# Four chained vision layers on one core: softmax sums partly by accumulating transfers, and inverse roots taken on compact tiles by way of memory

## The chip, the cores and the metric

The kernel runs on one core of one Trainium2 chip. The metric is the device time of one execution in microseconds. The core has a matrix engine (PE, with its weight loads shown apart as PEld), a vector engine (DVE), an activation engine (ACT), a general engine (POOL), and a sync engine (SP) that here does nothing but issue transfers. Each engine runs its own instructions strictly in the order in which the program lists them; they meet through semaphores. SBUF is the working memory, PSUM the eight banks into which PE writes, and DRAM the memory outside the core.

## What is computed

The input is 16 frames of 384 channels by 16 by 16 pixels, as two batches of eight frames. Four layers follow each other. All is in float32.

```python
# layer 0: attention of 12 heads of 32 channels over N = 2048 tokens of a batch
attn = softmax(einsum('bhnd,bhmd->bhnm', q * scale, k), axis=-1)
attn = alpha * eye + beta * attn - gamma * Cm        # Cm = 1/N everywhere
out = einsum('bhnm,bhmd->bhnd', attn, v)             # v is the input itself
# layer 1: 7x7 depthwise convolution, LayerNorm over channels, 384->1536, gelu,
y = (y - mu) * rsqrt(var + 1e-6) * ln_g + ln_b
y = gelu(y @ w1 + b1, approximate=False)
gx = sqrt(sum(y * y, axis=(1, 2)))                   # of each channel and frame
nx = gx / (mean(gx, axis=-1) + 1e-6)
y = (grn_g * (y * nx) + grn_b + y) @ w2 + b2         # 1536->384, and + residual
# layer 2: two Sobel filters, 768->384, LayerNorm, gelu, + residual
# layer 3: 1x1, 3x3 depthwise, 1x1, linear attention with phi(t) = exp((2t - t*t)/2),
#          projection, then LayerNorm, 384->1536, gelu, 1536->384, + residuals
```

## The kernel before

**Tiling.** A batch's 2048 tokens are four blocks of 512 (`BLK`). An activation is a tile of 128 partitions by 3 by 512. An attention *unit* is a batch and a group of four heads, so there are six units, each with four blocks of queries: 24 *blocks*. A block has 16 *steps* (`NQC`), one for every 128 keys.

**A step** (`unit`, lines 456 to 559). `scores` (463) makes four matmuls `st`, one per head, that run in four row groups of PE at the same time, and ACT takes their exponential into `e`. PSUM holds three double banks for this (`pst`, 412), so one ACT instruction covers two heads (1024 columns) and there are two of them in a step. `weighted` (481) is run one step later: four matmuls `av` multiply `e` by the values into one bank; DVE adds `e` to a running sum `s` (two `tensor_tensor` of 1024 columns). The sum over the 128 partitions is a matmul with ones, `dn`. How many steps DVE adds up before a `dn` is given for each block by `ADDS` (55): 16 means that DVE adds the whole block and PE makes one `dn`; 4 means four groups in a block, and all groups but the last are spread over later steps in four parts of 128 columns. `e` has 8 buffers of two heads and `s` has 4.

**The end of a block.** ACT copies `av` to `va`, and `xg` from the input. `finish` (536) reads `dn` with ACT into `r`; `due` then holds, for steps 2 to 5 of the next block, four reciprocals of 128 columns on DVE, at 6 and 7 the scaling and the store into the layer's output `l`, at 8 a check of the inverses on ACT. In step 5 (`SLOT`) of a block, `project` (569) makes two of the projections `p` that give queries and keys: six matmuls each, then an ACT copy.

**What fills the gaps.** `fill` (1481) is called after every step. It puts work of layer 1 among the attention's instructions: the convolution (49 DVE instructions per chunk, tile `y`) and the first parts of two layer 1 blocks ("leads"). `pace` (194) is a table by which it reckons what PE and DVE have in a step.

**The tail.** After attention, a planner (`Plan.all`, 180) puts all remaining work in one static order: it knows for every operation an engine, a length, what it comes after, and buffers; `RANK` (46) orders the tasks and `SLACK` (52) lets a better rank start later. `TURNS` (36) says which blocks use which pair of MLP weights one after the other; at every turn new weights (three tiles `wa`, three `wb`, 768 KB each) are loaded by SP.

**Normalizations.** `scaled` (916) makes the channel sum of squares by a matmul `sv` with ones, so that all 128 partitions hold the same row of 512 numbers; ACT takes the square root of 128x512, DVE the reciprocal of 128x512 in place, and DVE multiplies. It is called 24 times: by `layer1` (1012), `layer2` (1141) and `layer3c` (1421) for each of eight blocks. `layer1` also takes the root of `gx` (128x24) on ACT. ACT keeps one set of function tables at a time; roots, gelu and exp are in different sets here, and a load of tables stands between them.

Of the kernel before, what the change touches and what calls it, by code (L numbers as in the profile page):

```python
# [13 lines left out]
PSUM = bass.MemoryType.PSUM  # L14

# [16 lines left out]
SLOT = 5  # L32
# [4 lines left out]
    (0, ((0, 0), (0, 1), (0, 2), (0, 3),)),  # L37
    (1, ((0, 0), (0, 1),)),
    (0, ((1, 0), (1, 2),)),
    (1, ((0, 2),)),  # L40
    (0, ((1, 1), (1, 3),)),
    (1, ((1, 0), (0, 3), (1, 2), (1, 1), (1, 3),)),
# [4 lines left out]
    "mid": ((36.6, 22.0, 24.3, 85.6), (18.6, 42.9, 96.6, 26.9)),  # L47
    "l1": ((50.1, 89.5, 75.2, 4.0), (51.1, 16.8, 81.7, 28.5)),
    "l3c": ((45.7, 99.2, 100.9, 121.0), (-20.9, -6.3, 70.9, 62.0)),
    "conv": 109.4,  # L50
}
SLACK = 0.196
JUNK = 2

ADDS = (16, 8, 16, 16, 4, 4, 4, 2, 2, 8, 16, 16, 4, 16, 2, 4, 16, 8, 4, 4, 4, 4, 4, 4)
# [61 lines left out]
class Plan:  # L117
# [24 lines left out]
    def run(self, op):  # L142
        at = self.start(op)
        assert at is not None
        for tag, n in op.takes:
            del self.room[tag][:n]
        if op.engine == "PE" and at - self.free_at["PE"] > 2:
            at += 1.5
        if op.engine:
            self.free_at[op.engine] = at + op.length  # L150
        op.ready = at + op.length + op.lag
        for tag, n in op.gives:
            self.room[tag] = sorted(self.room[tag] + [op.ready] * n)
        if op.makes:
            self.made[op.makes] = op
        self.table = op.table or self.table
# [37 lines left out]
def pace(t):  # L194
# [3 lines left out]
    adds = ADDS[n]  # L198
    pe, dve = 2.066, 2.275 if t and i % adds else 0.0
    at = i - adds - 1  # L200
    parts = sum(j * adds // 4 == at % adds for j in range(4)) if at >= 0 else 0
    if parts:
        pe += 0.22 * parts
    elif i == 1 and n > 0:
        pe += 0.87
    else:
        pe += 0.09
    if n > 0:
        dve += {2: 0.88, 3: 0.88, 4: 0.88, 5: 0.88, 6: 0.6, 7: 0.66}.get(i, 0.0)
# [188 lines left out]
def attention(tc, X, xt, L0, block, small, col, cols, ones, load_qk, banks, fill, bound):  # L398
# [6 lines left out]
    with ExitStack() as actx:  # L405
# [3 lines left out]
        ep = pool("ep", 8)  # L409
        sp = pool("sp", 4)  # L410
        op = pool("op", 2)
        pst = pool("pst", 3, space=PSUM)
        pacc = pool("pacc", 1, space=PSUM)

        def bank2(name):
            return pst.tile([P, 2, BLK], F32, tag="st", name=name)

        banks.append(lambda name: bank2(name)[:, 0, :])
# [35 lines left out]
        due = {}  # L454

        def unit(u, made, gm):
# [3 lines left out]
            adds = ADDS[u * NBLK : (u + 1) * NBLK]  # L460
            acc, sums = {}, {}

            def scores(n, t):
                es = []
                for i in range(2):
                    es.append(ep.tile([P, 2, BLK], F32, tag="e", name=f"e_{u}_{n}_{t}_{i}"))
                sts = [bank2(f"st_{u}_{n}_{t}_{i}") for i in range(2)]
                for h in range(4):
                    rows = slice(HD * h, HD * (h + 1))
                    pe.matmul(  # L470
                        sts[h // 2][:, h % 2, :],
# [5 lines left out]
                for i in range(2):  # L477
                    act.activation(es[i], sts[i], AF.Exp, scale=HD**-0.5)
                return es

            def weighted(n, t, es):
                if t == 0:
                    acc["av"] = pacc.tile([P, BLK], F32, tag="av", name=f"av_{u}_{n}")
                for h in range(4):
# [3 lines left out]
                        es[h // 2][:, h % 2, :],  # L488
# [3 lines left out]
                at = t % adds[n]  # L492
                for i in range(2):
                    if at == 0:
                        sums[i] = es[i]
                    elif at == 1:
                        s = sp.tile([P, 2, BLK], F32, tag="s", name=f"s_{u}_{n}_{t}_{i}")
                        dve.tensor_tensor(s, sums[i], es[i], ALU.add)
                        sums[i] = s
                    else:  # L500
                        dve.tensor_tensor(sums[i], sums[i], es[i], ALU.add)


                k = (u * NBLK + n) * NQC + t
                if at == adds[n] - 1:
                    parts = 1 if t == NQC - 1 else 4
                    for i in range(parts):
                        due.setdefault(k + 2 + i * adds[n] // 4, []).append(
                            lambda i=i, summed=dict(sums): weights(
                                n, t, summed, ts(i, BLK // parts)  # L510
                            )
                        )
                for f in due.pop(k, ()):
                    f()
                if t == NQC - 1:
# [6 lines left out]
                    due[k + 2].append(lambda: finish(n, va, xg))  # L522

            def weights(n, t, summed, at):
                if t == adds[n] - 1 and at.start == 0:
                    acc["dn"] = pacc.tile([P, BLK], F32, tag="dn", name=f"dn_{u}_{n}")
                for h in range(4):
# [3 lines left out]
                        summed[h // 2][:, h % 2, at],  # L531
                        start=(t == adds[n] - 1 and at.start == 0),
# [3 lines left out]
            def finish(n, va, xg):  # L536
# [4 lines left out]
                r = op.tile([P, BLK], F32, tag="r", name=f"r_{u}_{n}")  # L541
                act.activation(r, acc["dn"], AF.Identity, accum_out=bound[:, 0, k : k + 1])

                def invert(i):
                    dve.reciprocal(r[:, ts(i, P)], r[:, ts(i, P)])
# [3 lines left out]

                def check():  # L550
# [1101 lines left out]
```

## Time and profile before

| what | us |
|---|---|
| median of three runs | 2679.3 (2674.36 to 2680.14) |
| the profiled execution | 2679.38 |
| its span, first to last instruction | 2677.6 |
| first score matmul of block 0 | 22.1 |
| last `dn` matmul of attention ends | 1052.4 |
| PE busy, of the span | 2644.6 |
| DVE busy | 2011.5 |
| ACT busy, of it 87 loads of tables | 1557.5, 111.6 |

A line of instruction groups reads: line, engine, operation, output <- inputs with their shapes, count, then busy time and the mean of one in ns, then idle time of the engine just before them and what ended it. All lines show line 96 because a helper there records every instruction; the tile names tell them apart. Where instructions of one engine follow each other, the next starts before the one before has ended, so that the sum of means is over the busy time.

Starts of score matmuls in the timeline give the time of each step. Blocks, from the start of one block's first `st` to the next one's:

| `ADDS` | blocks | us for a block with its two projections |
|---|---|---|
| 16 | 2, 3, 16 | 41.6 |
| 16 | 10, 11, 13 | 43.2, 42.2, 42.6 |
| 8 | 1, 9, 17 | 42.2, 42.2, 42.0 |
| 4 | 4, 5, 6, 12, 15, 18, 19 | 42.9 each |
| 2 | 7, 8, 14 | 46.1, 45.9, 45.8 |

Block 0 takes 40.6, block 20 44.1, block 21 (one projection) 41.9, and blocks 22 and 23 (none) 44.3 and 40.0. A step of a block with `ADDS` 16 takes 2.07 and 2.24 us in turn, one of `ADDS` 4 2.28, one of `ADDS` 2 2.50.

### The profile page before, as it was taken

To read this page: it belongs to the slowest core of one execution; us is meant where nothing else is said; L and a number is where in the kernel's file an instruction comes from. 1 tells how busy PE (TensorE), PEld (TensorE's weight loads), DVE (VectorE), ACT (ScalarE), POOL (GpSimd) and SP (SyncE) were. 2 spreads that over 40 slices of the span, in tenths; PEclk is the share of its full clock that TensorE was granted. 3 is DMA by queue.
4 is the path that set the end of the run, shared out by engine and by line. 5 is a ranking of instruction groups with operands and counts; after the bars stand their busy time and mean duration, and the time that the engine had idled before them with its cause. 6 is when DMAs were issued, how large, how long until landed. Compare 5 with 4: busy or idle time off the path is not lost. (4 is left out here: it accounts for less than half of the span.)

```text
span 2677.6 us, 32803 instructions
## 1 busy us (share of the span) xinstructions
PE 2644.6 (99%) x12997; PEld 1061.5 (40%) x12997; DVE 2011.5 (75%) x2588; ACT 1557.5 (58%) x2314; POOL 7.4 (0%) x54
## 2 busy tenths in 40 slices
PE   8999999999999999899999999999999999999999
PEld 2223333233323323345444454444444444454443
DVE  5999999999999889999999999999652202732300
ACT  6787878878787888564565335457443542625201
POOL 0000000000000000000000000000000000000000
PEclk9999999999999999999999999999999999999999
DMA  3000000000000003000001001011001110000000
GB/s 150 5 13 1 9 9 5 13 1 5 13 1 1 1 13 108 23 0 0 1 1 47 25 12 31 29 36 36 24 24 36 47 36 24 0 1 1 12 17 20
DMA packets 28851, 55.69 MB, mean 21 GB/s; under 512 B 1680, under 2 KB 14096, under 8 KB 28688
## 3 DMA queue, kind: packets, MB, share of 16 engines
q1 hardware_dynamic: 28544, 53.35, 6.0%
q8 instruction: 104, 1.70, 0.3%
q14 instruction: 59, 0.48, 0.1%
q10 hardware_dynamic: 144, 0.15, 0.0%
HBM read 47.21 MB, written 6.29 MB: 20 GB/s over the span
## 5 line engine op out<-in xcount | busy, mean ns | idle before, releaser
L96 ACT ACTIVATE e<-st 128x1024 f32<-128x1024 f32 x768 | 743.2, 1025 | 88.5 <-PE st L96 80.7
L96 DVE SCALAR_TENSOR_TENSOR y<-l,vec,y 128x420 f32<-128x420 f32 (+8 forms) x1152 | 660.0, 638 | 5.0
L96 DVE TENSOR_TENSOR s<-s,e 128x1024 f32<-128x1024 f32 x444 | 513.3, 1216 | 11.7 <-ACT e L96 11.2
L96 PE MATMUL st<-q,k 32*128 32x512 f32 x3072 | 474.1, 641 | 4.0 <-ACT e L96 2.3
L96 PE MATMUL av<-e,v 128*32 128x512 f32 x3072 | 410.9, 606 | 4.3 <-ACT va L96 4.2
L96 PE MATMUL ph_l<-y,wa 128*128 128x512 f32 x576 | 261.4, 597 | 0.0
L96 PE MATMUL ph_l3c<-d_l3c,wa 128*128 128x512 f32 x576 | 258.4, 593 | 0.0
L96 PE MATMUL po_l<-hid_l,wb 128*128 128x512 f32 x576 | 255.7, 596 | 1.1 <-ACT hid_l L96 1.1
L96 PE MATMUL po_l3c<-hid_l3c,wb 128*128 128x512 f32 x576 | 256.6, 593 | 0.0
L96 PEld LDWEIGHTS st<-q,k 32*128 32x128 f32 x3072 | 146.1, 183 | 220.1 <-issue 132.4
L96 DVE TENSOR_TENSOR s<-e,e 128x1024 f32<-128x1024 f32 x162 | 191.0, 1221 | 54.7 <-ACT e L96 36.0
L96 ACT ACTIVATE hid_l<-ph_l,vec 128x512 f32<-128x512 f32 x96 | 66.0, 687 | 202.9 <-PE ph_l L96 202.8
L96 ACT ACTIVATE hid_l3c<-ph_l3c,vec 128x512 f32<-128x512 f32 x96 | 65.6, 687 | 202.6 <-PE ph_l3c L96 202.5
L96 PEld LDWEIGHTS av<-e,v 128*32 128x32 f32 x3072 | 60.6, 108 | 298.1 <-issue 274.0
L96 DVE SCALAR_TENSOR_TENSOR o_l3c<-po_l3c,vec,l 128x512 f32<-128x512 f32 x24 | 17.5, 748 | 209.6 <-PE po_l3c L96 208.8
L96 PEld LDWEIGHTS po_l<-hid_l,wb 128*128 128x128 f32 x576 | 109.5, 191 | 139.1 <-issue 128.0
L96 PEld LDWEIGHTS ph_l3c<-d_l3c,wa 128*128 128x128 f32 x576 | 108.8, 190 | 137.2 <-issue 133.4
L96 PEld LDWEIGHTS ph_l<-y,wa 128*128 128x128 f32 x576 | 109.1, 191 | 136.0 <-issue 125.1
L96 PEld LDWEIGHTS po_l3c<-hid_l3c,wb 128*128 128x128 f32 x576 | 109.0, 190 | 134.6 <-issue 132.8
L96 PE MATMUL p<-x,wqk_sb 128*128 128x512 f32 x288 | 132.3, 610 | 1.2 <-DMA x<-in_x_dram 1.2
L96 DVE SCALAR_TENSOR_TENSOR g_l3a<-h_l3a,dw,g_l3a 128x450 f32<-128x450 f32 (+1 forms) x192 | 119.0, 702 | 4.2 <-ACT g_l3a L96 4.1
L96 PEld LDWEIGHTS dn<-s,ones 128*32 128x32 f32 x2016 | 64.1, 110 | 125.4 <-issue 107.0
(155 smaller groups left out, 2446.3 us busy)
## 6 DMA issues: line engine op xcount, KB each, us to landing
wa<-in_w_dram SPq DMA_DIRECT2D x9, 768.0 KB, 4.5
wb<-in_w_dram SPq DMA_DIRECT2D x9, 768.0 KB, 5.0
wa<-in_mlp_w_dram SPq DMA_DIRECT2D x9, 768.0 KB, 4.4
wb<-in_mlp_w_dram SPq DMA_DIRECT2D x9, 768.0 KB, 4.5
x<-in_x_dram SPq DMA_DIRECT2D x8, 768.0 KB, 10.6
v<-in_xt_dram SPq DMA_DIRECT2D x24, 256.0 KB, 2.7
out_dram<-o_l3c SPq DMA_DIRECT2D x24, 256.0 KB, 2.1
qkv<-in_qkv_wT_dram SPq DMA_DIRECT2D x3, 576.0 KB, 11.1
```

Source lines behind the costliest of these rows:

```text
L96: self.last = self.tc.keep_in_program_order(make(*args, **kw))
```

## The change

It has two parts.

**Attention.** PSUM becomes one pool of eight single banks; the exponential is taken per head (four ACT instructions of 512 columns per step) into one `e` tile of 2048 columns, with six buffers in place of `e` and `s`. Every block sums in groups of four steps: the second tile is added to the first by a transfer that accumulates, issued by POOL; the fourth to the third by DVE; and the two sums by DVE (`both`), one step later. `dn` follows in four parts from the third step after the group. What is due at the end of a block is put behind the next block's first step and its projections, which move from step 5 to step 0. The four reciprocals of 128x128 are replaced: one row of each head's `dn` (four partitions of 512) goes to DRAM and comes back as 128x16, is inverted there, goes to DRAM again, and four transfers spread each head's 512 numbers over 32 partitions.

**Normalizations.** ACT moves one row of `sv` (1x512) to SBUF; SP writes it to DRAM and reads it as 128x4; ACT takes logarithm and exp(-x/2); four small DVE instructions make a Newton step; SP writes it to DRAM and reads it back broadcast to 128 partitions. The root of `gx` is made the same way, without transfers. A table set that holds logarithm and exp is loaded by hand where the last one was gelu's.

The planner's lists (`TURNS` with eight turns in place of six, `RANK`, `SLACK`, `JUNK`), its lengths and `pace` are new, and `fill` lets an operation through that frees a bank.

```diff
+DRAM = bass.MemoryType.DRAM
-SLOT = 5
+PAIRED = (NB * NC - 1) * NBLK + 1
 TURNS = (
-    (0, ((0, 0), (0, 1), (0, 2), (0, 3),)),
-    (1, ((0, 0), (0, 1),)),
-    (0, ((1, 0), (1, 2),)),
-    (1, ((0, 2),)),
-    (0, ((1, 1), (1, 3),)),
-    (1, ((1, 0), (0, 3), (1, 2), (1, 1), (1, 3),)),
+    (0, ((0, 0), (0, 1), (0, 2),)),
+    (1, ((0, 0),)),
+    (0, ((0, 3), (1, 0),)),
+    (1, ((0, 2), (0, 1),)),
+    (0, ((1, 1), (1, 2),)),
+    (1, ((0, 3),)),
+    (0, ((1, 3),)),
+    (1, ((1, 0), (1, 1), (1, 3), (1, 2),)),
 )
...
-        ep = pool("ep", 8)
-        sp = pool("sp", 4)
+        ep = pool("ep", 6)
         op = pool("op", 2)
-        pst = pool("pst", 3, space=PSUM)
-        pacc = pool("pacc", 1, space=PSUM)
+        pb = pool("pb", 8, space=PSUM, reuse_waits="tile")
+        dp = pool("dp", 2, space=DRAM)
...
-                for i in range(2):
-                    act.activation(es[i], sts[i], AF.Exp, scale=HD**-0.5)
+                for h in range(4):
+                    act.activation(es[:, h, :], sts[h], AF.Exp, scale=HD**-0.5)
...
+                at = t % 4
+                if at % 2 == 0:
+                    acc[at] = es
+                elif at == 1:
+                    nc.gpsimd.dma_start(acc[0], es, accum_op=ALU.add)
+                else:
+                    dve.tensor_tensor(acc[2], acc[2], es, ALU.add)
+
+                    def both(summed=acc[0], other=acc[2]):
+                        dve.tensor_tensor(summed, summed, other, ALU.add)
+
+                    if end and block < PAIRED:
+                        late.append(both)
                     else:
...
+                        due.setdefault(k + 1, []).append(both)
+                    for i in range(1 if end else 4):
+                        f = lambda i=i, summed=acc[0]: weights(
+                            n, t, summed, ts(i, BLK if end else BLK // 4)
                         )
+                        when = k + 3 + i
+                        if block < PAIRED and when >= (block + 1) * NQC:
+                            late.append(f)
+                        else:
+                            due.setdefault(when, []).append(f)
...
-                def invert(i):
-                    dve.reciprocal(r[:, ts(i, P)], r[:, ts(i, P)])
+                sums = op.tile([P, BLK], F32, tag="sums", name=f"sums_{u}_{n}", bufs=1)
+                act.activation(sums, acc["dn"], AF.Identity, accum_out=bound[:, 0, k : k + 1])
+                away = dp.tile([4, BLK], F32, tag="away", name=f"away_{u}_{n}")
+                nc.sync.dma_start(away, sums[0:P:HD, :])
+                few = op.tile([P, BLK // HD], F32, tag="few", name=f"few_{u}_{n}")
+                nc.sync.dma_start(few, away.rearrange("h (j k) -> (h j) k", j=HD))
...
+                def invert():
+                    dve.reciprocal(few, few)
+                    back = dp.tile([P, BLK // HD], F32, tag="back", name=f"back_{u}_{n}")
+                    nc.sync.dma_start(back, few)
+                    for h in range(4):
+                        nc.sync.dma_start(
+                            r[ts(h, HD)],
+                            back[ts(h, HD)]
...
+                first = (k + 1) * NQC + (0 if k < PAIRED else 3)
+                for i, f in ((2, invert), (4, check), (6, scale), (7, put)):
+                    due.setdefault(first + i, []).append(f)
...
-                    if t == SLOT and steps:
-                        added = project(f"p_{u}_{n}", steps[:2])
-                        del steps[:2]
+                    if t == 0 and steps:
+                        many = 1 if len(steps) == NBLK - 1 else 2
+                        added = project(f"p_{u}_{n}", steps[:many])
+                        del steps[:many]
+                    for f in behind:
+                        f()
+                    behind.clear()
...
+    def exponent():
+        if table[0] != "exp":
+            table[0] = "exp"
+            act.preload_act_table_set("natural_log_exp_and_others")
+
+    def polish(r, v, name, n):
+
+        t = pools["few"].tile([P, n], F32, tag=f"t{n}", name=name)
+        dve.tensor_tensor(t, r, r, ALU.mult)
+        dve.tensor_tensor(t, t, v, ALU.mult)
+        dve.tensor_scalar(t, t, -0.5, 1.5, ALU.mult, ALU.add)
+        dve.tensor_tensor(r, r, t, ALU.mult)
...
-        a = scalar(BLK, 1, after=[m], gives=[("mm", 1)], table="sqrt")
-        yield a
-        act.activation(s[1], sv, AF.Sqrt, scale=1.0 / C, bias=eps)
-        a = Op("DVE", 3.27, after=[a])
-        yield a
-        dve.reciprocal(s[1], s[1])
+        a = scalar(BLK, 1, after=[m], gives=[("mm", 1)])
+        yield a
+        act.activation(s[1][:1], sv[:1], AF.Identity, scale=1.0 / C, bias=eps[:1])
+        a = Op("SP", 0.2, after=[a], lag=4.2)
+        yield a
+        away = memory.tile([1, BLK], F32, tag="away", name=f"away_{name}")
+        nc.sync.dma_start(away, s[1][:1])
+        v = pools["few"].tile([P, TB], F32, tag="v", name=f"v_{name}", bufs=2)
+        nc.sync.dma_start(v, away.rearrange("o (p k) -> (o p) k", k=TB))
+        a = Op("ACT", 0.5, after=[a], table="exp")
+        yield a
+        exponent()
+        r = pools["few"].tile([P, TB], F32, tag="r", name=f"r_{name}", bufs=2)
+        act.activation(r, v, AF.Ln)
+        act.activation(r, r, AF.Exp, scale=-0.5)
+        a = Op("DVE", 0.7, after=[a])
+        yield a
+        polish(r, v, f"t_{name}", TB)
+        a = Op("SP", 0.2, after=[a], lag=4.2)
+        yield a
+        back = memory.tile([P, TB], F32, tag="back", name=f"back_{name}")
+        nc.sync.dma_start(back, r)
+        nc.sync.dma_start(
+            s[1], back.rearrange("p k -> (p k)").unsqueeze(0).to_broadcast([P, BLK])
+        )
...
-        act.activation(gx, gx, AF.Sqrt)
+        act.activation(root, large, AF.Ln)
+        act.activation(root, root, AF.Exp, scale=-0.5)
...
+        polish(root, large, f"t_{n}", 2 * NFC)
+        dve.tensor_tensor(gx, gx, root.rearrange("p (k f) -> p k f", k=2), ALU.mult)
...
```

## The prediction

> **What bounds the kernel now.** The profiled execution has 2679.38 us (the median of the runs is 2679.3) and a span of 2677.6; 1.8 us lie around the span. I read the page's busy times and slices first.
>
> ```profile
> PE 2644.6 (99%) x12997; PEld 1061.5 (40%) x12997; DVE 2011.5 (75%) x2588; ACT 1557.5 (58%) x2314; POOL 7.4 (0%) x54
> ...
> DVE  5999999999999889999999999999652202732300
> ```
>
> PE is busy 99% of the span; DVE's slices are full for two thirds of it; POOL does almost nothing. Next the windows: attention (22 to 1050), then four stretches of the tail. Columns: length, then busy time of PE, PEld, DVE, ACT, POOL, granted clock, share of the DMA engines, GB/s.
>
> ```profile
> 22.00:1050.00 1028.00, 1019.67 (x8403) 317.80 (x8406) 961.36 (x1012) 836.08 (x990) 0.00 (x0) 1.00 0.03 8
> 1050.00:1300.00 250.00, 239.18 (x673) 108.75 (x669) 239.06 (x370) 141.70 (x297) 0.85 (x6) 0.97 0.10 35
> 1300.00:1700.00 400.00, 398.51 (x1141) 181.84 (x1130) 390.36 (x605) 188.85 (x343) 1.70 (x12) 1.00 0.07 20
> 1700.00:2000.00 300.00, 299.73 (x902) 139.93 (x901) 249.14 (x378) 152.72 (x279) 1.70 (x12) 1.00 0.11 32
> 2000.00:2678.00 678.00, 671.40 (x1864) 306.11 (x1862) 168.33 (x207) 234.20 (x402) 2.49 (x18) 1.00 0.06 19
> ```
>
> DVE is nearly full in attention and until 1700, but PE is full in every row, so time freed on DVE is worth only what PE loses by waiting for it. PE's named waits in the tail, all of them 12.4 us, begin with these:
>
> ```profile
> PE su_l L96 <- DVE s_l L96: 3.6, 1, 3.6
> PE sv_l L96 <- DVE gmean_l L96: 2.1, 1, 2.1
> PE zb_l3b L96 <- DVE z_l3b L96: 2.1, 2, 1.5
> PE pg_l L96 <- DVE gs_l L96: 1.9, 1, 1.9
> ```
>
> In attention the waits are inside "busy": the timeline shows them as later starts. First the turn from block 19 to 20 (`ADDS` 4), then three starts in block 3 (`ADDS` 16).
>
> ```profile
> 879.86 1.14 PE L96 MATMUL st<-q,k 32*128 32x512 f32 x8
> 881.03 1.94 ACT L96 ACTIVATE e<-st 128x1024 f32<-128x1024 f32 x2 [0.34 <-PE st L96]
> 882.14 1.14 PE L96 MATMUL st<-q,k 32*128 32x512 f32 x8
> 882.85 0.61 ACT L96 ACTIVATE va<-av 128x512 f32<-128x512 f32 x1
> 883.33 0.82 ACT L96 ACTIVATE xg<-x,gm,vec 128x512 f32<-128x512 f32 x1
> 883.51 1.07 PE L96 MATMUL av<-e,v 128*32 128x512 f32 x8 [0.23 <-ACT va L96]
> ```
>
> ```profile
> 168.50 1.31 PE L96 MATMUL st<-q,k 32*128 32x512 f32 x8
> 170.74 1.14 PE L96 MATMUL st<-q,k 32*128 32x512 f32 x8
> ```
>
> A step with a quarter of a `dn` takes 882.14 - 879.86 = 2.28; one without takes 2.07, and every other time 170.74 - 168.50 = 2.24, because half of its `st` waits for ACT to free a double bank. An `ADDS` 2 step, with two quarters, takes 2.50, so a quarter costs PE (2.50 - 2.07)/2 = 0.217. At the turn, `va` and `xg` hold up ACT, and PE with it.
>
> **The change, part by part.** Durations are from these rows:
>
> ```profile
> L96 ACT ACTIVATE e<-st 128x1024 f32<-128x1024 f32 x768 | 743.2, 1025 | 88.5 <-PE st L96 80.7
> L96 ACT COPY k<-p 128x512 f32<-128x512 f32 x24 | 13.6, 591 | 36.2 <-PE p L96 36.2
> L96 DVE TENSOR_TENSOR s<-s,e 128x1024 f32<-128x1024 f32 x444 | 513.3, 1216 | 11.7 <-ACT e L96 11.2
> L96 DVE RECIPROCAL r<-r 128x128 f32<-128x128 f32 x96 | 88.7, 939 | 6.0 <-ACT r L96 6.0
> L96 DVE RECIPROCAL s_l<-s_l 128x512 f32<-128x512 f32 x16 | 53.6, 3348 | 20.7 <-ACT s_l L96 20.6
> ```
>
> *Sums on PE.* `ADDS` gives 7x1 + 3x2 + 11x4 + 3x8 = 81 groups; now there are 24x4 = 96. That is 15 x 0.87 = 13 us more for PE, on the path. Every block becomes like one of `ADDS` 4, which takes 42.9 with its two projections. A projection pair costs 7.41 - 2.24 = 5.2 (step 5 against the step before). Blocks 0 to 20 have a pair, block 21 half of one, 22 and 23 none: 24 x 42.9 - 2.5 x 5.2 = 1016.6 against 1028.2 as measured, **-11.6**. This already takes all stalls out of blocks 20 to 23, which stand 11.7 over it where the two leads wait for roots, their table loads and reciprocals. The leads remain, though without those: half comes back, **+6** (bounds 0 and 11.7).
>
> *The turn.* An `ADDS` 4 block needs of PE 16 x 2.07 + 12 x 0.217 + 1.0 (last `dn`) + 5.2 = 41.9, so 1.0 of its 42.9 is stall, mostly at the turn. Moved to step 0, the projections give PE 5.2 us just there. ACT has in that step some 2.1 of exponentials, 0.5 + 0.7 for `va` and `xg`, 1.0 for two copies and 0.8 for the sums, 5.1 in all, under some 9 of PE. Nearly all of 21.5 blocks' stall goes: **-20** (bounds -21.5 and 0). The copies queue behind `xg`, but nothing needs them before the next step.
>
> *Exponentials per head.* Two instructions of 1024 take 1.94. Two `k` copies of 512 in a row start 0.48 apart and one lasts 0.59, so four of 512 take 0.59 + 3 x 0.49 = 2.06: +0.12 per step, about 2 us per block, on an ACT that is busy 34.4 of 43.0 in block 5. Costed at 0; if overlap fails it is 4 x 0.6 = 2.4 per step (second rival). A single bank comes free twice as often, which may take the 0.17 out of the alternate steps: up to 4 steps x 0.09 x 24 = -8, kept for the range.
>
> *DVE.* 606 additions of 1024 (704 us) become 192 of 2048, at 2.3 (two of 1024 in a row) 442; 96 reciprocals (88.7) become 24 of 16 columns, about 4. DVE gets 347 us in attention. `fill` can bring convolution forward (159 of 697 us of tile `y` lie in attention now), but in the tail that is worth only PE's waits. The three around 1085 to 1095, 7.7 us, stand where convolution is the last to finish: **-8** (bounds -12.4 and 0).
>
> *The accumulating transfer.* 96 transfers of 1 MB, which no row shows. 256 KB of `v` land in 2.7 and 768 KB of `wa` in 4.5, so 512 KB cost 1.8 and 1 MB lands in 5.4; if the target is read as well, 2 MB of traffic give 9.0. POOL is idle in attention (0.00) and hides the issue. DVE's `both` queues behind it from three steps later. The sum tile is held until its last `dn`, so that of six `e` tiles the transfer's source is wanted again for the exponential three to four steps on: three steps are 3 x 2.28 = 6.9. I take 6.2, nearer the lower end because the 16 DMA engines are 3% busy: hidden, 0. Beyond 6.9, ACT waits in its queue, the `st` banks are not freed and PE stalls.
>
> The Trainium skill ("DMA: Bandwidth & Descriptors", section on the anatomy of one DMA on the gpsimd path) gives 2.0 us plus bytes over 436 GB/s for a plain transfer on this path, 4.4 for 1 MB as an estimate by its fit; it has no price for the accumulation, and the 768 KB row here (4.5) is already longer than its 3.8. By the page the transfer is hidden with 2.5 us to spare; by the doubled row it is not hidden.
>
> *Sums by way of DRAM.* One ACT read, two transfers, one small reciprocal, then five transfers. The nearest are 256 KB rows, 2.1 (`out`) and 2.7 (`v`): at most 4.8 for each round trip. The reciprocal stands two steps after the sums and may wait some 0.5 us on DVE, which has room; scaling stands four steps later (9 us). On SP only `v` loads queue behind, wanted a block later. 0.
>
> *Normalizations.* 24 times, DVE gives back 3.35 - 0.65 (four instructions of about 0.16), 65 us; the chain grows from 0.69 + 3.35 = 4.0 to 0.6 + 4.8 + 0.45 + 0.65 + 4.4 = 10.9. Table loads (87 x 1.28) stay near their number, off the path. What hides the added 6.9 is other blocks' matmuls, placed ahead of the waiting ones. 12 more weight loads of 768 KB share SP's queue. Taken as 0; bounds -5 and third rival.
>
> *Sum:* 2677.6 - 11.6 + 6 - 20 - 8 = 2644.0, with 1.8 around it 2646.
>
> **The rivals.**
> 1. *Slower: the accumulating transfer is late.* It decides from 6.9 us; at 9.0, 96 x 2.1 = +202: 2848. The gain of 34 is used up at 7.25. For it: the buffers leave no fourth step for certain; against: idle DMA engines.
> 2. *ACT takes the place.* At 2.4 a step, 16 x 2.4 + 3.4 (ACT's other work in block 5) + 0.5 = 42.3 of ACT per block, 1015, and with the turn's 1.0 kept 1039 against 1028: +11 - 8 + 1.8, 2682. For it: waits stand before each of the four; against: `k` copies overlap.
> 3. *Round trips show.* 22 normalizations lie in the tail; if half of their added 6.9 ends on PE, +76: 2722. PE loses the gain from 5 exposed ones. For it: static order, transfers behind weight loads on one queue; against: 1.6 ms of matmuls to cover with.
>
> **How the numbers follow.** Forecast 0.66, own range 2630 (both bounds of turn and waits, and the alternate steps in part) to 2668 (half the turn, no gain in the tail, leads as before); first rival 0.12, second 0.13, third 0.09. About 0.2% (5 us) is what a measurement here tells from no change: 2674 to 2685. Faster: 0.66 + 0.03 of the second + 0.01 of the third = 0.70; same: 0.06 of the second; slower: 0.12 + 0.04 + 0.08 = 0.24. The range 2620 to 2715 leaves out the first rival, half of the third, and 0.03 below.
>
> **What will show it.** Steps with a quarter `dn` at 2.28 and a first step of about 9 us; attention ending near 1026 in place of 1052; no wait of ACT `e` or of `st` on a transfer; the accumulating transfer landing under 6.9; DVE below 75% in attention without convolution; fewer waits at the start of the tail. I am wrong if ACT's `e` rows wait for the transfer or ACT shows no idle time in attention, or if PE's waits on normalized tiles exceed 30 us in the tail.

## The result, and the profile after

The changed kernel takes 2802.6 us (median of four runs, 2799.4 to 2806.0) against 2679.2 before (2674.4 to 2680.1): a ratio of 1.0465 with a 95% interval of 1.0444 to 1.0485. It is **slower by 4.6%**, outside the range of the prediction and on the other side of it. The profiled execution has a span of 2798.1 us against 2677.6.

The page's busy times and DVE's slices come first.

```profile
PE 2725.6 (97%) x13477; PEld 1100.3 (39%) x13477; DVE 1630.4 (58%) x2222; ACT 1609.3 (58%) x3135; POOL 90.1 (3%) x150
...
DVE  3686846876444554399999778599712316316020
```

DVE lost 381 us of work, as meant, and its slices in attention fell to 4 to 8. The span grew all the same. The windows say where (columns as before: length, PE, PEld, DVE, ACT, POOL, granted clock, share of the DMA engines, GB/s); attention now ends at 1132.7, not at 1052.4.

```profile
22.00:1128.00 1106.00, 1092.16 (x8898) 354.14 (x8890) 662.06 (x575) 877.51 (x1768) 82.73 (x96) 0.99 0.51 105
1128.00:1400.00 272.00, 252.56 (x693) 114.47 (x694) 223.39 (x387) 137.09 (x301) 0.97 (x7) 0.97 0.13 42
1400.00:1800.00 400.00, 389.89 (x1101) 177.34 (x1100) 320.00 (x557) 221.43 (x408) 1.96 (x14) 1.00 0.14 39
1800.00:2100.00 300.00, 294.51 (x787) 133.01 (x786) 222.38 (x398) 137.51 (x265) 0.42 (x3) 1.00 0.11 32
2100.00:2798.00 698.00, 680.78 (x1970) 314.25 (x1968) 199.34 (x287) 230.11 (x387) 3.32 (x24) 0.99 0.09 26
```

The DMA engines went from 3% to 51% of attention. In the tail PE is no longer full: 35 us of the three windows from 1128 to 2100 and 17 of the last are idle. The first of PE's named waits from the end of attention on, which now come to 41 us in place of 12.4:

```profile
PE po_l L97 <- ACT hid_l L97: 13.3, 8, 3.6
PE pg_l L97 <- DVE gs_l L97: 9.1, 3, 5.3
PE zb_l3b L97 <- DVE z_l3b L97: 5.3, 2, 3.3
PE pc_l3a L97 <- DVE l L97: 4.1, 3, 2.6
```

I divide each span at two instructions: the first `st` and the end of the last `dn`. (The first expectations below give 1104 and 1670 for the changed kernel, divided a few microseconds earlier.)

| | before | after | difference |
|---|---|---|---|
| start to first `st` | 22.1 | 21.7 | -0.4 |
| **attention** (first `st` to last `dn`) | 1030.3 | 1111.0 | **+80.7** |
| **tail** (last `dn` to the end) | 1625.2 | 1665.4 | **+40.2** |
| time at half TensorE clock, attention / tail | 6.8 / 13.7 | 34.1 / 27.3 | +27.3 / +13.6 |

**Where attention stalls.** Added up from its undisturbed steps, a block would now take 42.5 us; but from block 1 to 21 each takes 44 to 51. The first step of a block takes 9.06 in most, as foreseen. Then the starts of the steps stand apart by 2.07 to 2.36 in most blocks until step 9, and by 2.9 to 6.5 at step 10 in 19 of blocks 1 to 20; about half are late at step 11 too, and some at 14 and 15. Block 12 is the worst (50.6). First its transfers: the issues on POOL's queue that add, and the queue of SP.

```profile
583.95 0.86 POOL L496 DMA_DIRECT2D e<-e  x1 [16.14 <-PE st L97]
592.91 0.86 POOL L496 DMA_DIRECT2D e<-e  x1 [8.09 <-ACT bit L97]
```

```profile
584.97 0.32 SPq L559 DMA_DIRECT2D back<-few  x1
592.97 1.84 SPq L561 DMA_DIRECT2D r<-back  x4
```

`back` is 8 KB. It is issued 1.0 us after a 1 MB transfer and lands only when that has landed: 8.0 us. The broadcast `r<-back` then goes out beside the second 1 MB transfer. Now the engines, from the timeline of the same stretch:

```profile
600.67 2.82 PE L97 MATMUL st<-q,k 32*128 32x512 f32 x8
601.23 2.06 ACT L97 ACTIVATE e<-st 128x512 f32<-128x512 f32 x4 [1.91 <-DMA e<-e]
601.42 0.69 DVE L97 TENSOR_TENSOR va<-va,r 128x512 f32<-128x512 f32 x1 [4.50 <-DMA r<-back]
...
606.19 2.06 ACT L97 ACTIVATE e<-st 128x512 f32<-128x512 f32 x4 [2.90 <-DVE e L97]
...
606.84 2.17 PE L97 MATMUL st<-q,k 32*128 32x512 f32 x4 [1.08 <-ACT e L97]
...
608.94 1.93 PE L97 MATMUL av<-e,v 128*32 128x512 f32 x8
```

Three things in a row. ACT can't write its next `e` tile, because the transfer still reads the buffer (1.91). DVE stands 4.50 before `va*r`, so its additions behind it are late and ACT waits again for a tile that DVE holds (2.90). PE stalls twice, and then eight `av` matmuls take 1.93 us in place of 1.07: the clock is granted by half, here for 6.8 us from 607.75.

The rows that the prediction priced, and the section of DMA issues (KB of one, median us from issue to landing):

```profile
L97 ACT ACTIVATE e<-st 128x512 f32<-128x512 f32 x1536 | 790.0, 614 | 149.3 <-PE st L97 62.2
L97 DVE TENSOR_TENSOR e<-e,e 128x2048 f32<-128x2048 f32 x192 | 439.9, 2291 | 294.5 <-ACT e L97 143.5
```

```profile
e<-e POOLq DMA_DIRECT2D x96, 1024.0 KB, 7.3
```

### The profile page after: what moved, and what is told of

Read it like the earlier page. It is cut to its first block, busy times and chain, and to the rows that moved or that the text cites. A ratio compares the mean times of both kernels' runs of the same rounds, so it can differ in the third digit from the quotient of the medians.

```text
span 2798.1 us, 34238 instructions
## 1 busy us (share of the span) xinstructions
PE 2725.6 (97%) x13477; PEld 1100.3 (39%) x13477; DVE 1630.4 (58%) x2222; ACT 1609.3 (58%) x3135; POOL 90.1 (3%) x150
## 5 line engine op out<-in xcount | busy, mean ns | idle before, releaser
L97 ACT ACTIVATE e<-st 128x512 f32<-128x512 f32 x1536 | 790.0, 614 | 149.3 <-PE st L97 62.2
L97 DVE TENSOR_TENSOR e<-e,e 128x2048 f32<-128x2048 f32 x192 | 439.9, 2291 | 294.5 <-ACT e L97 143.5
L97 PE MATMUL st<-q,k 32*128 32x512 f32 x3072 | 509.3, 646 | 12.6 <-ACT e L97 11.8
L97 PE MATMUL av<-e,v 128*32 128x512 f32 x3072 | 430.4, 612 | 0.0
L97 PEld LDWEIGHTS st<-q,k 32*128 32x128 f32 x3072 | 153.4, 184 | 228.4 <-issue 147.4
L97 PEld LDWEIGHTS av<-e,v 128*32 128x32 f32 x3072 | 71.5, 108 | 299.9 <-issue 277.7
L97 PEld LDWEIGHTS dn<-e,ones 128*32 128x32 f32 x2496 | 81.7, 111 | 168.9 <-issue 156.3
L97 PE MATMUL dn<-e,ones 128*32 128x128 f32 (+1 forms) x2496 | 139.6, 302 | 4.0 <-DVE e L97 4.0
```

What stands on the lines that cost most here:

```text
L97: self.last = self.tc.keep_in_program_order(make(*args, **kw))
```

## The experiments

Each kernel is the changed one but for its edit, unless it is said otherwise. Attention and tail are measured as in the table above. They are always those of one execution, and so is the time where no ratio is given; four executions of the changed kernel span 6.6 us.

### Attention: the transfers that add

**Additions on DVE.** The 96 transfers become additions of DVE; all else stays.

```
-    pe, dve = 2.125, 2.35 if i % 4 == 3 or i % 4 == 0 and t > 4 else 0.0
+    pe, dve = 2.125, 2.35 if i % 4 in (1, 3) or i % 4 == 0 and t > 4 else 0.0
...
-    nc.gpsimd.dma_start(acc[0], es, accum_op=ALU.add)
+    dve.tensor_tensor(acc[0], acc[0], es, ALU.add)
```

> The accumulating transfer is replaced by a third DVE addition of 2048 columns per group; the rest is the changed kernel. Attention, from the first score matmul to the end of the last one's block, takes 1104 us in the changed kernel, and its own undisturbed steps add up to about 1007. Theory A (transfers: the accumulating one is late for the reuse of its source tile, alone or because it meets the small ones): attention near 1015, total 2700 to 2720. Theory B (four exponentials per step make ACT the bound, transfers only look guilty): attention stays within 15 us of 1104, total 2790 or more. DVE gets 96 x 2.29 = 220 us more and stays under 85% in attention.

Measured 2719.3 us: attention 1032.1, tail 1663.0. The transfers account for 78.9 of attention's 80.7 us, and for next to nothing of the tail. But 1032.1 is above the 1015 expected and also 1.8 above before's attention: without its main fault the change still brings none of the 26 us that the prediction counted on there.

**The inverses on DVE again.** `r` is inverted in place by four reciprocals, as before, without the way through DRAM; the transfers that add stay.

```
-    nc.sync.dma_start(away, sums[0:P:HD, :])
-    nc.sync.dma_start(few, away.rearrange("h (j k) -> (h j) k", j=HD))
...
-        dve.reciprocal(few, few)
...
+    def invert(i):
+        dve.reciprocal(r[:, ts(i, P)], r[:, ts(i, P)])
```

> The accumulating transfers stay; the inverses of the sums are taken as before the change, by four reciprocals of 128 columns on DVE, with no transfers. Theory A1 (the two kinds of transfer collide: the small ones wait behind 1 MB, and their broadcast makes the next accumulation land after 7.6 to 8.9 us in place of 6.6): attention falls from 1104 to 1020 to 1035, accumulations of a block's second group land at 6.7. Theory A2 (6.6 us by itself is too late): attention stays over 1080.

Measured 2764.8: attention 1083.6. The round trips cost 27 us beside the transfers. It is their meeting that costs: DVE waits 48.6 us in all for the broadcast `r<-back` after the change, and in the run without transfers never, until attention has ended. But with the round trips gone ACT still waits 42.0 us on the transfers (53.6 after), and attention is 51 above the run without transfers (ACT's waits in attention: total, times, longest):

```profile
ACT e L97 <- DMA e<-e: 42.0, 32, 3.0
```

The transfer is too long by itself: with nothing else moving it lands 6.9 us after its issue (the 22 of the 96 after the change that had no other packet beside them: 6.9 to 7.0).

**A seventh `e` tile.** What the transfer reads is then wanted again one step later. Room for it comes from smaller buffers for `va`, `xg`, `r` and the means.

```
-        ep = pool("ep", 6)
+        ep = pool("ep", 7)
...
-                    va = op.tile([P, BLK], F32, tag="va", name=f"va_{u}_{n}")
+                    va = op.tile([P, BLK], F32, tag="va", name=f"va_{u}_{n}", bufs=1)
```

> The changed kernel with a seventh tile for the exponentials; room for it comes from single buffers for the two copies at a block's end, one shared for sums and inverses, and the channel means' scratch put into another pool. All transfers stay. Theory A2 (what costs is that the accumulation's source tile is wanted again about 6.5 us after the issue, while it takes 6.6 alone and up to 8.9 beside others): one more step, 2.28 us, covers 6.6 to 8.7, ACT's waits on the transfer fall from 53.6 us to under 10, attention from 1111 to 1035 to 1055. If attention stays over 1090, the reuse of the tile is not what costs, and the late sums on DVE are.

Measured 2750.0: attention 1064.5, 46.5 less than after, though not the 1035 to 1055 expected. Waits of ACT in attention (total, times, longest), after and then with the seventh tile:

```profile
ACT e L97 <- DMA e<-e: 53.6, 34, 3.1
...
ACT e L97 <- DVE e L97: 25.9, 29, 3.4
```

```profile
ACT e L97 <- DVE e L97: 8.2, 3, 3.0
...
ACT e L97 <- DMA e<-e: 2.3, 3, 0.8
```

The transfers take just as long (median 7.3). So the loss isn't their length alone but the **buffer's deadline**: from issue to the exponential that wants the buffer. A block has four transfers. For the second it is three steps, some 6.5 us, and for the third 6.8; the first has 8.3 and the fourth over 13 in most blocks, because the turn follows. So of ACT's 34 waits after the change 32 stand at steps 9 and 13. Most blocks fell to between 42.6 and 44; blocks 1, 2, 5, 12 and 13 stayed at 47 to 50. These are the blocks in which DVE stands longest before `va*r`, 4.4 to 8.3 us, for a late broadcast (3.8 at most in the other blocks up to 22; total, times, longest):

```profile
DVE va L97 <- DMA r<-back: 46.6, 15, 8.3
```

In each of them ACT or PE then waits 2.3 to 4.7 us for something that DVE makes late. By these rows, what the seventh tile leaves is the round trips' share; a seventh tile without round trips was not tried.

**Scaling later.** `va*r` and what follows at steps 10 and 11 in place of 6 and 7, so that a late `r` holds up nothing on DVE.

```
-    for i, f in ((2, invert), (4, check), (6, scale), (7, put)):
+    for i, f in ((2, invert), (4, check), (10, scale), (11, put)):
```

> Scaling and store of a block's output move from steps 6 and 7 to steps 10 and 11; all transfers stay as they are. If DVE standing before the scaling, with additions queued behind it, is what makes the exponential wait, attention falls by 30 us or more (to 1075 or less). If the second accumulation landing late is enough by itself, it falls by less than 20.

Measured 2786.9: attention 1098.0, 13 less than after. With six tiles, DVE's standing is the smaller part.

**The changed attention in the frame of before.** For these two the kernel is the one before, with its pacing of side work, lists and normalizations; only the attention is the changed one. From the end of attention every PE, ACT and DVE instruction stands in the order of before. First with the transfers, then with all additions on DVE, in groups of 16, 8, 4 or 2.

> The same frame of before, but attention exactly as changed, with the transfers that add. Tail instructions in the order of before. Theory A (the transfers cost attention about 80 us, and nothing of the tail's +40 is theirs): attention 1100 to 1125 us, tail 1617 to 1633, time 2745 to 2775. Rival B (attention's loss shrinks once DVE also has the side work of before, or the tail grows with it): attention below 1090, or a tail above 1640.

```
-    nc.gpsimd.dma_start(acc[0], es, accum_op=ALU.add)
+    dve.tensor_tensor(acc[0], acc[0], es, ALU.add)
...
+GROUPS = (16, 8, 8, 8, 8, 4, 4, 2, 2, 8, 8, 8, 8, 8, 2, 4, 8, 8, 4, 4, 4, 4, 4, 4)
```

> The kernel before with the changed attention alone (single-bank scores, turns with the projections at their first step, inverses compact by way of memory), with every addition on DVE in groups of 16, 8, 4 or 2 and no transfer that adds. Pacing of the side work, lists and normalizations are those of before, and from the end of attention on every PE, ACT and DVE instruction stands in the order of before. Theory A (attention gains once the transfers are gone, and the tail's loss is its order alone): attention 1000 to 1018 us (groups of eight took 41.6 a block in the run with groups of eight, against 42.9 for a block of before), tail 1617 to 1633 us, time 2645 to 2672. Rival B (the tail loses after the changed attention whatever its order): tail above 1640. Rival C (the gain of the run with groups of eight came from its lighter side work): attention above 1025.

With transfers 2759.2: attention 1098.9, tail 1635.6. Without them 2707.8 (ratio 1.0115, 1.0098 to 1.0132): attention 1048.5, tail 1633.2. The two lie 50 us apart here too, though with the transfers every block has groups of four, so that the groups differ as well. The tail is 8 to 10 longer than before's though its order is the same, and the two traces, laid over each other instruction by instruction, differ in one place only, 25 to 45 us behind the seam; from there on they run together within 1 us. The waits in that place, in the run without transfers:

```profile
PE su_l L98 <- DVE s_l L98: 10.5, 1, 10.5
...
DVE few L98 <- DMA few<-away: 7.2, 1, 7.2
```

After the last block nothing is left to cover the round trip, and DVE, in program order, has the tail's first work behind it. That attention was 1048.5 met the third reading of the expectation, not the first. I took it that side work paced for other groups of additions falls where DVE has no room, and tried that next.

**Paced as before, and the seam mended.** The same kernel with the groups that the pacing supposes, and the last block's inverse in place on DVE.

```
+GROUPS = (4,) + ADDS[1:]
...
+    if k == NB * NC * NBLK - 1:
+        def invert():
+            for i in range(TB):
+                dve.reciprocal(r[:, ts(i, P)], r[:, ts(i, P)])
```

> The run of the changed attention in the old frame with two faults of that run mended: the additions go in the groups that the pacing of the side work supposes (those of before; the first block in groups of 4, as no side work is paced there), and the last block's inverse is taken in place by four reciprocals, as before, in place of the round trip that DVE waited 7.2 us for at the seam. Theory A (side work out of pace cost attention some 30 us there, and the round trip at the seam the tail's 8 us): attention 1003 to 1020, tail 1622 to 1628, time 2650 to 2672, faster than before by 0.3 to 1.1%. Rival B (the changed attention has no gain to give beside the side work of before): attention above 1028. Rival C (the tail's 8 us come from something other than that round trip): tail 1631 or more.

Measured 2691.7 (ratio 1.0046, 1.0032 to 1.0059): the tail is 1625.6, before's to half a microsecond, so the seam is settled. Attention is 1041.9 and misses its 1003 to 1020: groups that fit the pacing are worth 6.6 us, not some 30. Its blocks without much side work are short (40.7 with a group of 16, before 41.6), but two cost 46.5. The timeline at the start of block 17 shows why:

```profile
754.72 14.27 DVE L98 TENSOR_TENSOR e<-e,e 128x2048 f32<-128x2048 f32 x6
...
760.64 5.42 PE L98 MATMUL p<-x,wqk_sb 128*128 128x512 f32 x12
...
769.05 1.93 PE L98 MATMUL dn<-e,ones 128*32 128x512 f32 x8 [2.99 <-DVE e L98]
```

The changed turn sums the last group straight after the projections. Before, that came two steps into the next block, so DVE could carry a lag over the turn; now PE waits for it, and a stretch of 3.4 us at half clock follows (from 768.9). These two blocks make 9 of the 11.6 us over before; that the order at the turn is the cause was not tried.

### The tail: normalizations or order

**Old normalizations under the new lists.**

```
-        act.activation(r, v, AF.Ln)
-        act.activation(r, r, AF.Exp, scale=-0.5)
...
-        polish(r, v, f"t_{name}", TB)
...
+        act.activation(s[1], sv, AF.Sqrt, scale=1.0 / C, bias=eps)
...
+        dve.reciprocal(s[1], s[1])
```

> The 24 normalizations and the eight roots of layer 1 are made as before the change (root on ACT, reciprocal of 128x512 on DVE); attention, the turns and the ranks are those of the changed kernel. The tail, from the end of attention to the end of the span, takes 1670 us in the changed kernel and 1627 before. If the longer chains over memory cost the 43 us, the tail falls to 1640 or less; if the new turns and ranks cost them, it stays at 1655 or more. Attention stays near 1104.

Measured 2826.0: attention 1115.3, tail 1686.8, 21 more than after. Taken alone that would say that the new normalizations gain.

**Old and new normalizations under the old lists**, both with the additions on DVE (`TURNS`, `RANK`, `SLACK` of before).

```
-SLACK = 0.326
+SLACK = 0.196
...
-    "conv": 111.6,
+    "conv": 109.4,
```

> The third DVE addition in place of the transfer, as in the first run, with normalizations, turns, ranks and slack of before the change. Attention near 1032 as there; the tail, 1663 there and 1625 before the change, comes back to 1620 to 1635, so the total is 2670 to 2685. If the tail stays over 1650, attention's new end costs it, not the normalizations or the lists.

> As the run before it, but with the new normalizations (chains over memory) under the turns, ranks and slack of before the change (scratch of one tile as in the changed kernel). If the longer chains cost the tail its 38 us, the tail is 1655 or more, whatever lists; if the new lists cost them, it falls to 1640 or less. With the old normalizations under the new lists the tail was 1687, so I expect it over 1655.

Measured 2805.8 and 2810.1: attention 1039.5 and 1032.7, tails 1742.7 and 1754.1. The first has before's normalizations and before's lists, and loses 118 us against before's tail: I had expected it near before's. Which side work attention leaves undone differs, and the lists no longer fit: the planner's ends in the table below say the same.

**The new normalizations alone, in the kernel before.**

```
-        dve.reciprocal(s[1], s[1])
...
+        act.activation(r, v, AF.Ln)
+        act.activation(r, r, AF.Exp, scale=-0.5)
...
+        polish(r, v, f"t_{name}", TB)
```

> The kernel before with the changed normalizations alone (inverse roots compact by way of memory, from logarithm and exponential with a Newton step, and the root of the squares likewise); attention, its additions, pacing and lists are those of before. The order of the tail's instructions follows from the changed durations. Theory A (the normalizations as such gain or cost little, as predicted: -8 us): attention 1028 to 1034, tail 1605 to 1630. Rival B (the longer chain of the normalizations is what costs the tail 40 us): tail 1645 to 1690 us, with the excess in PE's waits on normalized tiles. Rival C (under lists made for other durations the order goes wrong): tail above 1700 with over 60 us at the half clock.

Measured 2794.8: attention 1023.8, tail 1746.6. That is the third reading: not the waits on normalized tiles, but an order gone wrong, with 116 us at half clock. A window of this run (columns as above) has PE idle for 71 us and a granted clock of 0.90:

```profile
1700.00:2100.00 400.00, 329.24 (x1014) 149.97 (x1014) 278.49 (x469) 159.59 (x294) 1.69 (x12) 0.90 0.09 23
```

The tail's order is worked out by the kernel's own planner, which also knows the end that it expects. I read that off for the kernels that had run, then searched for other `RANK` and `SLACK` (some 1100 tries each) by that end, and ran two of what came out: the change relisted (the diff shows some of its lists), and the change with old normalizations relisted.

```
-    "l1": ((8.0, 41.0, 68.6, 34.5), (68.2, 7.5, 43.5, 63.0)),
+    "l1": ((-92.4, 79.5, -7.1, -80.3), (35.0, -186.6, 58.5, -96.5)),
...
-    "conv": 111.6,
+    "conv": 183.3,
...
-SLACK = 0.326
+SLACK = 0.366
```

> The changed kernel with other lists alone (ranks and slack found by a search of some 1100 tries for the end that the kernel's own planner works out for the tail: 1617.8 us against 1630.5 with its lists; before: 1602.1). Measured tails of the runs so far lie 15 to 35 us above the planner's end. Theory A (the tail's loss is mostly the order that the lists give): tail 1645 to 1657 (1665 less 13, give or take 6), attention 1111 +- 8, time 2782 to 2800. Rival B (the new normalizations cost time that the planner does not see, so that another order gains nothing): tail 1660 or more.

> The changed kernel with the normalizations of before and lists searched for in the same way and number of tries (planner's end 1622.3 us, against 1617.8 for the new normalizations relisted). Theory A (the two normalizations are worth the same to the tail once each has lists of its own): tail within 12 us of the relisted change's, 1640 to 1660. Rival B (the new normalizations cost the tail 15 us or more, unseen by the planner): this tail at least 12 us below the relisted change's. Rival C (they gain): at least 12 us above it.

Measured 2778.9 and 2782.9: attention 1115.5 and 1118.7, tails **1639.3 and 1640.8**. With one search of equal length for each, the two normalizations are worth the same to the tail, and 26 of its 40 us are the order alone. All tails beside the planner's end:

| kernel | planner's end | tail measured |
|---|---|---|
| before | 1602.1 | 1625.2 |
| groups and lists (last run below) | 1602.1 | 1624.1 |
| change relisted | 1617.8 | 1639.3 |
| old normalizations relisted | 1622.3 | 1640.8 |
| after | 1630.5 | 1665.4 |
| groups of eight, old lists | 1632.3 | 1664.5 |
| old normalizations, new lists | 1671.7 | 1686.8 |
| new normalizations alone, old lists | 1715.8 | 1746.6 |
| additions on DVE, old normalizations and lists | 1724.7 | 1742.7 |
| additions on DVE, new normalizations, old lists | 1734.5 | 1754.1 |

The measured tail lies 15 to 35 us above, over a spread of 130. Of the change's +40, 28 stood in its planner's end.

### A kernel that beats both

**Groups of eight.** Old normalizations and lists, the changed attention, and DVE adding 8 tiles to a sum.

```
-    nc.gpsimd.dma_start(acc[0], es, accum_op=ALU.add)
+    dve.tensor_tensor(acc[0], acc[0], es, ALU.add)
...
+ADDS = (16,) + (8,) * 19 + (4,) * 4
```

> As the run with the old tail, but DVE adds up eight steps per group (16 in block 0, 4 in the last four blocks), so that PE makes two groups of sums fewer in 19 blocks: 19 x 2 x 0.87 = 33 us less. DVE then has 14 x 2.29 = 32 of some 41 us per block, beside convolution. If PE bounds attention, it takes 1000 to 1010, total 2645 to 2655, under the 2677 of before; if DVE bounds it, attention stays at 1025 or more.

Measured 2692.3: attention 1004.1, tail 1664.5. For the first time attention gained, 26 us, but the tail paid for it.

**Groups and lists.** The same with the first block and two others in groups of 4, the mended seam, and groups and lists searched for by the planner's end (1602.1).

```
-ADDS = (16,) + (8,) * 19 + (4,) * 4
+ADDS = (4, 8, 8, 8, 8, 8, 8, 8, 8, 4, 8, 8, 8, 8, 8, 4, 8, 8, 8, 8, 4, 4, 4, 4)
```

> The run with groups of eight again (changed attention, all additions on DVE, normalizations of before), with three changes: the first block and two others in groups of 4 (so that side work fits as the planner supposes), the last block's inverse in place by four reciprocals, and lists found by a search for the end that the planner works out (1602.1 us against 1632.3; before: 1602.1). Theory A (side work that fits its pace, a seam without the round trip, and a tail that follows the planner's end with some 23 us on top, as before): attention 996 to 1008, tail 1620 to 1636, time 2640 to 2668, faster than before by 0.4 to 1.5%. Rival B (attention's gain with groups of eight was bought with side work left to the tail): tail above 1645 or attention above 1025, not faster. What this tells of the prediction: whether its gain in attention was there to be had at all.

Measured **2657.1 us against 2677.4: ratio 0.9925, 0.9911 to 0.9938**. Attention is 1007.4 and the tail 1624.1. The page and its attention window:

```profile
PE 2626.2 (99%) x12389; PEld 1048.0 (39%) x12389; DVE 1980.4 (75%) x2235; ACT 1599.5 (60%) x3083; POOL 7.4 (0%) x54
...
PEclk9999999999999999999999999999999999999999
```

```profile
22.00:1026.00 1004.00, 1002.53 (x7789) 304.40 (x7788) 929.37 (x659) 877.16 (x1757) 0.00 (x0) 1.00 0.05 15
```

PE is full in attention, without a stretch at half clock. The single banks, the new turn and the compact inverses (but for the last block's) are in it, though what each is worth was not tried; neither the transfers that add nor the new normalizations are.

## Why the prediction was wrong

*The accumulating transfer* is the step that failed. It was taken as 6.2 us against a deadline of three steps, 6.9, and so as hidden. It lands in 6.9 alone and 7.3 in the median, up to 9.3. The deadline is some 6.5 where it is shortest, because the transfer goes out a little behind the start of the three steps and not all of them carry a quarter of `dn`. So it is late even alone. The sign that the prediction named showed: ACT's `e` rows wait for it, 53.6 us in all. The first rival had the mechanism and the formula: by its own sum (landing less deadline) 96 x (7.3 - 6.5) gives 77 us, where 79 were measured. That agreement is luck: only two of a block's four transfers have a deadline that short, and each stall drags late additions and half speed behind it. The mistake was to choose a value inside bounds of 5.4 to 9.0 "because the 16 DMA engines are 3% busy": that was the share of before, and the change itself brings them to 51%.

*Sums by way of DRAM* failed in the same way. At most 4.8 was allowed for each round trip, from rows of transfers that had the engines to themselves. Here the 8 KB write alone took 8.0 in block 12. SP waits for it 23 times and DVE for its broadcast 14 times (total, times, longest):

```profile
SPq L561 <- DMA back<-few: 112.4, 23, 7.6
```

```profile
DVE va L97 <- DMA r<-back: 48.6, 14, 6.5
```

The run without the round trips puts 27 us on both round trips together. The Trainium skill ("DMA: Bandwidth & Descriptors", section "Issuing engines are not separate DMA queues") says that transfers started by different engines run on the same 16 DMA engines and interleave. The rows agree, and go further: the small write all but waited for the whole of the large one. The rule spoke against pricing the two apart.

*The order of the tail* was no term of the sum at all. The normalizations were priced at 0 and that held (1639.3 against 1640.8). But new durations and new side work make a new order, and that cost some 26 of the tail's 40. The seam's 8 to 10, shown in the frame of before, which the third rival had in kind (a round trip that nothing covers) though not in place, may make up most of the rest; in the changed kernel the seam was not tried by itself.

*Sums on PE and the leads* (-11.6 and +6): the quarter of 0.217 held, steps with one take 2.28. That the leads lose half of their stall held in the kernel before with the new normalizations (attention 1023.8 for 1030.3, all of it in block 22). It didn't in the changed attention: there blocks 20 to 23 take 176 us to the last `dn` without transfers, before 173, where the terms make 165. Why stays open. *The turn* (-20) was mis-sized. Every other step still takes 2.18, and without transfers an undisturbed block takes 42.6 for 42.9, -0.3 and not -1.0. The new turn has the price shown above besides: DVE's lag is no longer carried over. Without transfers attention gained nothing: 1032.1, where these terms made 1030.3 - 11.6 + 6 - 20 = 1004.7. Of these 27 us some 13 are the turn's, 0.6 in each of the first 20 blocks, 11 the last four blocks' and 3 block 10's. That such a gain is to be had is shown by the last run (1007.4), but by larger groups of additions on DVE, which no longer has the reciprocals to do there.

The turn from block 19 to 20 after the change, to set beside that of before:

```profile
946.10 1.14 PE L97 MATMUL st<-q,k 32*128 32x512 f32 x8
...
948.38 2.84 PE L97 MATMUL p<-x,wqk_sb 128*128 128x512 f32 x6
...
949.18 0.63 ACT L97 ACTIVATE va<-av 128x512 f32<-128x512 f32 x1
...
949.66 0.84 ACT L97 ACTIVATE xg<-x,gm,vec 128x512 f32<-128x512 f32 x1
...
951.16 0.64 PE L97 MATMUL dn<-e,ones 128*32 128x128 f32 x16
...
952.01 1.06 PE L97 MATMUL dn<-e,ones 128*32 128x512 f32 x8 [0.21 <-DVE e L97]
...
953.00 1.14 PE L97 MATMUL st<-q,k 32*128 32x512 f32 x8
```

`va` and `xg` now run under the projection (one, as block 20 has half a pair), as foreseen.

*Exponentials per head* held: four take 2.06, to the digit. The second rival falls with it.

*DVE's relief* (-8): the size of the time freed held roughly (381 us in all, where 347 and 65 were counted), its use didn't. "`fill` can bring convolution forward" misread the code: it stops after the first `YB` blocks of convolution, so tile `y` has 187 us in attention where it had 159, and the rest of the freed time stands idle.

## What to carry to other kernels

Price a transfer with the traffic that the change itself adds, and against the step at which its buffer is really wanted, counted from the order of buffers: 34 waits of 1.6 us in the mean, with late additions and the lower clock behind them, outweighed all that was gained. Where a static order is planned from durations, the planner's own end is a term of the sum: any change of a duration or of what is left over shifts it, here by up to 130 us, and it can be read before anything runs: every tail measured here lay 15 to 35 us above it. And before moving work to an idle engine, ask what bounds now: PE was full, and most of the 381 us taken off DVE, 75% busy before, only became idle time of DVE.

## What the hardware showed that was not expected

- A 1 MB transfer within SBUF that adds lands 6.9 us after its issue on otherwise idle engines; its first packet starts 1.4 after it and its last ends at 6.6. As an estimate by the fit of the Trainium skill ("DMA: Bandwidth & Descriptors", section on the anatomy of one DMA on the gpsimd path) a plain transfer of that size takes 4.4; the measurement decides for this kind.
- Of the 96, 29 had no other data beside them but a packet or two of the instruction queues. In 11 of these the last packet ended after 8.0 to 8.3 us, in 18 after 6.6 to 7.4; in the 22 with nothing beside them after 6.6 to 6.7. That these packets are the cause was not tried.
- The granted clock falls to 0.5 during or just after a stretch of 0.7 to 5.3 us in which PE stands idle, here for 3.41, 6.83 or 10.24 us each time, 61 us in all after the change. In the three tails whose order went wrong it is 116 to 126 us, and up to 44.4 at a time. Half of that time is lost. The Trainium skill ("TensorE: Matmul & The Clock Gate", section "Part 1: The HAM clock gate") gives two states and a window of 3413 ns that decides between them. The lengths agree, all being whole numbers of such windows. But the page has the clock fall after an idle window, and here it fell with PE busy for up to 79% of the 3.41 us before; the measurement decides.
